# A four-layer convolution chain: first gram matrix from row loads and transposes, second image's gram rows two steps later, and final loads placed in the stages' own tiles

## The chip, the cores and the metric

The kernel runs on one core of one Trainium2 chip. The metric is the device time of one execution in microseconds (us); lower is better. Everything is float32.

## The reference

The input x has 16 images of 64 channels and 128 x 128 pixels. Four layers follow one another, each of the form x = x + layer(groupnorm(x)), with 32 groups of 2 channels:

```python
# layer 0: gram matrix per image, then a 1x1 convolution
gram = jnp.einsum('bcn,bdn->bcd', xf, xf) / N          # xf: (B, C, H*W), N = H*W
y = jnp.einsum('bcd,bdn->bcn', gram, xf)
out = jnp.einsum('oc,bchw->bohw', conv_w, y)
# layer 1: two fixed 3x3 edge filters per channel
out = jnp.abs(y[:, 0]) + jnp.abs(y[:, 1])
# layer 2: shift a quarter of the channels left, a quarter right, then a 3x3 convolution plus bias
# layer 3: 3x3 convolution, 1x1 convolution, batch norm over ALL images, leaky relu
y = (y - mean) * jax.lax.rsqrt(var + EPS)
return jnp.clip(jnp.where(y >= 0, y, LEAK * y), 0.0, CEIL)
```

Two facts order the whole program. The gram matrix of an image needs all of that image before layer 0 can start on it. The batch norm of layer 3 needs all sixteen images before the last element-wise pass can start on any of them.

## The kernel before, in words

Every image passes through four stages, each a small class whose method `at(i, q)` issues the work for row block i (8 of them, each 8 rows of both image halves) in quarter q of a step.

- `Gram` (lines 407 to 444) computes the gram matrix. It loads x with pixels on the partitions (`xr`, eight loads of 512 KB in runs of one 128-pixel row, 512 bytes), ScalarE copies each into `xw`, and TensorE takes 128 products of 64 x 65 from `xw`. Then `gram_chain` (lines 301 to 405) runs some fifty tiny operations that end in the mixing matrix `abd` and the normalisation numbers `co` of layer 1.
- `Front` (lines 450 to 566) loads x again in rows (`x`, two loads of 256 KB per block, 4 KB runs), mixes it with `abd` on TensorE (`po`), normalises it into `xh` on ScalarE, does layer 1 on VectorE (`u`, `e`) and stores x2 to device memory.
- `Layer2` (lines 625 to 770) loads x2 back (`v2`), forms differences and products, and stores x3 (`x3_d`). The x3 tiles stay on chip too: ten buffers named `x3`.
- `Layer3` (lines 773 to 857) uses the x3 tiles, forms differences, products and y, accumulates the sums for the batch norm, and stores y (`y_d`, four stores of 128 KB per block from a ring of two `y` tiles).

The order is written out by hand: `keep_in_program_order` (line 72) keeps every instruction of the five engine wrappers in the order in which Python issues it, so each engine has one fixed list. The line of almost all instructions in the profile is therefore 72, and groups are told apart by tile names. The order of steps stands in lines 861 to 900: `starts` sets Front, Layer2 and Layer3 of image b at steps 15 + 8b, 25 + 8b and 35 + 8b (with some lead), and `pace` sets `Gram`: image 0 from step 0, images 1 to 6 at double speed from step 12 on, every fourth step, later images every eighth. `tick` advances the small chains by one link each quarter step.

SP issues almost all transfers, from one list in program order. The transfers rotate over eight completion semaphores, and in the built program each transfer waits for the one eight before it.

After the last stage all pools are closed. The batch norm's numbers follow (lines 905 to 928: `mv`, `pm_bn`, ..., `sc`, `sh`), and then the end: a new pool `io` with six buffers each of `yt` and `rt`, 64 parts of 1 MB, four of them loaded ahead:

```python
    for n, (b, q) in enumerate(parts):
        fetch(n + 4)
        yt, rt = loaded.pop(n)
        act.activation(yt, yt, AF.Relu, bias=sh, scale=sc)
        dve.scalar_tensor_tensor(rt, yt, 255.0, rt, op0=ALU.min, op1=ALU.add)
        sp.dma_start(whole(out[b].rearrange("c h w -> (c h w)"), q), rt)
```

Of the kernel before, what the change touches and what calls it, by code (L numbers as in the profile page):

```python
# [9 lines left out]
F32 = mybir.dt.float32  # L10
# [5 lines left out]
P = 128  # L16
# [91 lines left out]
def tile_kernel(ctx: ExitStack, tc: tile.TileContext, x, cw_h, w2_t, b2, wbin_t, w1_t, b1, gamma, beta, consts, out):  # L108
# [9 lines left out]
    nc.sync.dma_start(kc, consts)  # L118
# [4 lines left out]
    def load_const(src, shape, name):  # L123
        t = cpool.tile(shape, F32, name=name)
        nc.sync.dma_start(t, src)
        return t

    cwh = load_const(cw_h, [P, C], "cwh")
    b2_sb = load_const(b2, [P, 1], "b2_sb")
    b1_sb = load_const(b1, [P, 1], "b1_sb")  # L130
    gamma_sb = load_const(gamma, [P, 1], "gamma_sb")
    beta_sb = load_const(beta, [P, 1], "beta_sb")
# [24 lines left out]
    with ExitStack() as ph:  # L157
        wpool = ph.enter_context(tc.tile_pool(name="wpool", bufs=1))
        xin = ph.enter_context(tc.tile_pool(name="xin", bufs=2))
        work = ph.enter_context(tc.tile_pool(name="work", bufs=2))  # L160
        ring = ph.enter_context(tc.tile_pool(name="ring", bufs=2))
        stp = ph.enter_context(tc.tile_pool(name="stp", bufs=2))
        ps_two = ph.enter_context(tc.tile_pool(name="ps_two", bufs=2, space=PSUM))
        ps_one = ph.enter_context(tc.tile_pool(name="ps_one", bufs=1, space=PSUM))
        ps_po = ph.enter_context(tc.tile_pool(name="ps_po", bufs=1, space=PSUM))
        ps_g = ph.enter_context(tc.tile_pool(name="ps_g", bufs=1, space=PSUM))
        ps_sm = ph.enter_context(tc.tile_pool(name="ps_sm", bufs=1, space=PSUM))

        def sv(name, n=1):
            return small.tile([P, n], F32, tag=name, name=name)  # L170

        def cols(o):
            return slice(o * C, (o + 1) * C)

        last = [1]

        def small_product(dst, wt, src):

            for o in (1 - last[0], last[0]):
                pe.matmul(dst[cols(o)], wt[:, cols(o)], src, start=True, stop=True)  # L180
            last[0] = o


        bank = ps_sm.tile([P, 512], F32, name="bank")
        turn = [0]

        def sm(n, rows=P):
            if n > 8:
                return bank[0:rows, P:P + n]
            turn[0] = (turn[0] + 1) % 16  # L190
            return bank[0:rows, 8 * turn[0]:8 * turn[0] + n]
# [3 lines left out]
        xw = wpool.tile([P, W // 2, C + 1, 2], F32, name="xw")  # L195
        nc.gpsimd.memset(xw[:, :, C, :], 1.0)

        xh = wpool.tile([P, 3, R + 2, W + 2], F32, name="xh")
        nc.gpsimd.memset(xh, 0.0)
        junk = wpool.tile([P, R * W], mybir.dt.bfloat16, name="junk")  # L200
        wbd = wpool.tile([P, P], F32, name="wbd")
        nc.gpsimd.memset(wbd, 0.0)

        w2 = wpool.tile([P, 3, 3, P], F32, name="w2")
        w3 = wpool.tile([P, 3, 3, P], F32, name="w3")
        nc.gpsimd.memset(w2, 0.0)
        nc.gpsimd.memset(w3, 0.0)
        for slot, i, o, ky in TO_SLOTS:
            nc.scalar.dma_start(w2[i * C:(i + 1) * C, slot, :, o * C:(o + 1) * C], w2_t[:, ky])

        wm = wpool.tile([P, 3, P], F32, name="wm")
        for n in range(2):
            o = 1 - single(TO_SLOTS, n)[0]
            nc.vector.tensor_copy(wm[:, :, cols(o)], w2[:, n, :, cols(o)])
        w0 = wpool.tile([P, P], F32, name="w0")
        nc.gpsimd.memset(w0, 0.0)

        wb = work.tile([P, R + 1, W + 2], F32, tag="u", name="wb")
        wb = flat(wb)[0:C, 0:9 * C].rearrange("p (y x c) -> p y x c", y=3, x=3)
        w1 = work.tile([P, R, W + 2], F32, tag="e", name="w1", bufs=1)[0:C, 0, 0:C]  # L220
        nc.scalar.dma_start(wb, wbin_t)
        nc.scalar.dma_start(w1, w1_t)
        for ky in range(3):
            pw = sm(3 * C, rows=C).rearrange("p (k c) -> p k c", k=3)
            for kx in range(3):
                nc.tensor.matmul(pw[:, kx, :], wb[:, ky, kx, :], w1, start=True, stop=True)
            for slot, i, o, kk in TO_PAIRS:
                if kk == ky:
                    nc.vector.tensor_copy(w3[i * C:(i + 1) * C, slot, :, o * C:(o + 1) * C], pw)

        packed = {}
        for name, w, table in (("pk2", w2, TO_SLOTS), ("pk3", w3, TO_PAIRS)):
            nc.vector.tensor_add(w[:, 2], w[:, 0], w[:, 1])
            packed[name] = wpool.tile([P, 2, C], F32, name=name)
            for n in range(2):
                o, i = single(table, n)
                for kx, half in ((1, i), (0, 1 - i)):
                    nc.vector.tensor_copy(
                        packed[name][half * C:(half + 1) * C, n], w[i * C:(i + 1) * C, n, kx, o * C:(o + 1) * C]
                    )  # L240

        diffs, twins = {}, {}
        for name in ("d2", "d3"):
            diffs[name] = wpool.tile([P, 2, CP, W + 2], F32, name=name)
            nc.gpsimd.memset(diffs[name], 0.0)
            twins[name] = wpool.tile([P, 2, CP, W + 2], F32, name=f"q{name}")
            nc.gpsimd.memset(twins[name], 0.0)


        chains = []  # L250

        def tick():
            for c in list(chains):
                if next(c, chains) is chains:
                    chains.remove(c)

        def rstd(mE, eps):

            me = sv("me", 2)
            dve.tensor_copy(me, mE)  # L260
            nv = sv("nv")
            dve.scalar_tensor_tensor(nv, me[:, 0:1], me[:, 0:1], me[:, 1:2], op0=ALU.mult, op1=ALU.subtract)
            var = sv("var")
            dve.tensor_scalar(var, nv, -1.0, eps, op0=ALU.mult, op1=ALU.add)
            sd = sv("sd")
            act.activation(sd, var, AF.Sqrt)
            yield
            r0 = sv("r0")
            dve.reciprocal(r0, sd)

            e = sv("e")
            dve.scalar_tensor_tensor(e, var, r0, r0, op0=ALU.mult, op1=ALU.mult)
            dve.tensor_scalar(e, e, -0.5, 1.5, op0=ALU.mult, op1=ALU.add)
            r = sv("r")
            dve.tensor_mul(r, r0, e)
            return r, me[:, 0:1]

        def coefficients(st, put, back=None):

            s2 = sv("s2", 2)  # L280
            dve.tensor_reduce(s2, st, axis=AX.X, op=ALU.add)
            yield
            pm = sm(2)
            small_product(pm, k("gmean"), s2)
            yield
            r, mean = yield from rstd(pm, GN_EPS)
            co = sv("co", 2) if back is None else sv("co2", 6)
            dve.tensor_copy(co[:, 0:1], r)
            dve.scalar_tensor_tensor(co[:, 1:2], mean, -1.0, r, op0=ALU.mult, op1=ALU.mult)
            if back is not None:  # L290

                dve.reciprocal(co[:, 2:3], r)
                dve.tensor_mul(co[:, 3:4], co[:, 2:3], k("left"))
                dve.tensor_mul(co[:, 4:5], co[:, 2:3], k("right"))
                dve.tensor_add(co[:, 5:6], mean, back)
            put(co)


        lead = {}

        def gram_chain(b, pg):

            gs = stp.tile([P, C + 1], F32, tag="gs", name=f"gs_{b}", bufs=1)
            dve.tensor_copy(gs, pg)
            if b > 1:
                yield
            gd = sm(C + 1)
            small_product(gd, k("same"), gs)
            yield
            g = stp.tile([P, C + 1], F32, tag="g", name=f"g_{b}", bufs=1)  # L310
            dve.tensor_scalar_mul(g, gd, 1.0 / HW)
            mu = g[:, C:C + 1]
            st = sv("st0", 2)
            dve.tensor_copy(st[:, 0:1], mu)
            junk0 = stp.tile([P, C], F32, tag="junk0", name=f"junk0_{b}", bufs=1)
            dve.scalar_tensor_tensor(
                junk0, g[:, 0:C], 1.0, k("Id"), op0=ALU.mult, op1=ALU.mult, accum_out=st[:, 1:2]
            )
            if b > 1:
                yield  # L320
            pm = sm(2)
            small_product(pm, k("gavg"), st)
            yield
            r, mean = yield from rstd(pm, GN_EPS)
# [7 lines left out]
            if b > 1:  # L332
                yield
# [660 lines left out]
```

## Time and profile before

| what | value |
|---|---|
| median of three runs | 2853.81 us (2851.17 to 2856.24) |
| the profiled execution's own time | 2855.78 us |
| its span, first to last instruction | 2854.0 us |
| TensorE busy | 2238.3 us (78% of the span) |
| VectorE busy | 2193.6 us (77%) |
| ScalarE busy | 2101.5 us (74%) |
| GpSimd busy | 886.8 us (31%) |
| bytes moved by DMA | 685.91 MB, mean 240 GB/s |
| granted TensorE clock, mean | 0.893 |

The page cuts the span into 40 slices of 71 us; each digit is the busy share of a slice in tenths. The chain of waits is followed back from the last instruction to whatever released each step. A window's row gives the busy time of each engine in one stretch, the granted TensorE clock, the mean share of the 16 DMA engines, and GB/s. PE is TensorE's matmul, PEld its weight load, DVE VectorE, ACT ScalarE, POOL GpSimd, SP SyncE.

### The profile page before, as it was taken

How to read it: one execution, taken by the hardware profiler on the slowest of the kernel's cores; microseconds unless marked ns; L12 is line 12 of the kernel's file. 1: busy time of each engine (PE TensorE's matmuls, PEld its weight loads, DVE VectorE, ACT ScalarE, POOL GpSimd, SP SyncE). 2: the span in 40 equal slices, each digit the busy share in tenths (PEclk: the TensorE clock that was granted, in tenths of full speed). 3: DMA queues.
4: the chain of work that ended last, by engine and by line, in shares of the span. 5: the costliest groups of instructions: out<-in, count | busy, mean ns of one | idle time of the engine just before them, and what ended most of it. 6: DMA issues, size and time to landing. Idle time of an engine off the chain costs nothing. (4 is left out here: it accounts for less than half of the span.)

```text
span 2854.0 us, 45849 instructions
## 1 busy us (share of the span) xinstructions
PE 2238.3 (78%) x14772; PEld 1166.6 (41%) x14772; DVE 2193.6 (77%) x3694; ACT 2101.5 (74%) x3107; POOL 886.8 (31%) x1326
## 2 busy tenths in 40 slices
PE   3568899999999999999999999999999992000000
PEld 2333444545463635363635453566666640000000
DVE  3999999898989898989898989999995333332332
ACT  4666779888889898888898979899996674222222
POOL 1045434343434343434333434444443300000000
PEclk8678999999999999999999999999999996555555
DMA  6788978888888888888888867888877528999999
GB/s 164 191 221 225 234 199 239 215 224 215 220 216 221 218 221 217 216 216 216 220 220 217 214 178 193 211 209 209 211 199 185 145 71 320 426 426 426 426 426 394
DMA packets 661229, 685.91 MB, mean 240 GB/s; under 512 B 58672, under 2 KB 587072, under 8 KB 636416
## 3 DMA queue, kind: packets, MB, share of 16 engines
q1 hardware_dynamic: 635008, 614.41, 72.7%
q0 software_dynamic: 24576, 68.12, 9.8%
q8 instruction: 119, 1.95, 0.3%
q14 instruction: 118, 0.97, 0.1%
q10 hardware_dynamic: 1408, 0.46, 0.1%
HBM read 346.23 MB, written 268.44 MB: 215 GB/s over the span
## 5 line engine op out<-in xcount | busy, mean ns | idle before, releaser
L72 PE MATMUL two<-d,w 128*64 128x508 f32 (+2 forms) x2560 | 890.5, 586 | 0.0
L72 PE MATMUL two<-d,wi 128*64 128x508 f32 (+3 forms) x1536 | 619.7, 577 | 0.0
L72 POOL DMA_DIRECT2D qd<-d x512 | 270.3, 530 | 868.9 <-issue 312.7
L72 PE MATMUL two<-qd,pk 128*64 128x512 f32 (+1 forms) x1024 | 518.9, 588 | 6.3 <-DMA qd<-d 5.8
L72 POOL TENSOR_SCALAR edges<-v,co 64x8 f32<-64x8 f32 x512 | 355.3, 694 | 358.9 <-ACT v L72 266.7
L72 PEld LDWEIGHTS two<-d,w 128*64 128x64 f32 x2560 | 306.2, 136 | 275.7 <-issue 188.8
L72 PE MATMUL po<-x,abd 128*64 128x512 f32 x1024 | 367.9, 628 | 56.9 <-ACT xh L72 55.9
L72 DVE TENSOR_TENSOR d<-v 128x512 f32<-128x512 f32 (+1 forms) x512 | 346.8, 680 | 76.2 <-issue 36.9
L72 DVE SCALAR_TENSOR_TENSOR rt<-yt,rt 128x2048 f32<-128x2048 f32 x64 | 146.7, 2292 | 321.3 <-DMA rt<-x_d 321.3
L72 PE MATMUL one<-v,w 128*64 128x508 f32 (+2 forms) x1600 | 392.7, 578 | 0.0
L72 PE MATMUL one<-v,wi 128*64 128x508 f32 (+3 forms) x1536 | 391.1, 593 | 0.0
L72 ACT ACTIVATE yt<-yt,sh,sc 128x2048 f32<-128x2048 f32 x64 | 134.1, 2095 | 332.7 <-DMA yt<-y_d 332.7
L72 ACT COPY qd<-d 64x512 f32<-64x512 f32 x512 | 316.0, 617 | 20.9 <-DVE d L72 14.5
L72 DVE SCALAR_TENSOR_TENSOR e<-e 128x1032 f32<-128x1032 f32 (+1 forms) x256 | 313.4, 1224 | 0.0
L72 ACT ACTIVATE xh<-po,co 128x128 f32<-128x128 f32 (+1 forms) x480 | 275.6, 622 | 39.5 <-PE po L72 37.4
L72 PEld LDWEIGHTS two<-d,wi 128*64 128x64 f32 x1536 | 195.8, 135 | 145.8 <-issue 96.3
L72 DVE SCALAR_TENSOR_TENSOR y<-two,c 128x1024 f32<-128x1024 f32 x128 | 156.1, 1220 | 122.7 <-ACT v L72 65.7
L72 POOL TENSOR_SCALAR v<-v,kc 128x9 f32<-128x9 f32 x256 | 245.1, 971 | 12.0
L72 PEld LDWEIGHTS one<-v,w 128*64 128x64 f32 x1600 | 172.7, 137 | 157.1 <-issue 92.6
L72 ACT ACTIVATE v<-x,co 128x512 f32<-128x512 f32 (+2 forms) x368 | 235.6, 707 | 0.0
L72 PEld LDWEIGHTS one<-v,wi 128*64 128x64 f32 x1536 | 164.9, 139 | 152.4 <-issue 106.4
L72 ACT ACTIVATE u<-u 128x1024 f32<-128x1024 f32 x128 | 135.7, 1060 | 96.1 <-DVE u L72 95.8
(136 smaller groups left out, 3455.2 us busy)
## 6 DMA issues: line engine op xcount, KB each, us to landing
xr<-in_x SPq DMA_DIRECT2D x128, 512.0 KB, 6.9
x<-in_x SPq DMA_DIRECT2D x256, 256.0 KB, 4.2
x_d<-u SPq DMA_DIRECT2D x512, 128.0 KB, 3.6
y_d<-y SPq DMA_DIRECT2D x512, 128.0 KB, 4.2
yt<-y_d SPq DMA_DIRECT2D x64, 1024.0 KB, 16.2
rt<-x_d SPq DMA_DIRECT2D x64, 1024.0 KB, 12.3
out<-rt SPq DMA_DIRECT2D x64, 1024.0 KB, 14.4
x_d<-x SPq DMA_DIRECT2D x496, 128.0 KB, 2.5
```

The source lines that it names most:

```text
L72: return self.tc.keep_in_program_order(call(*args, **kwargs))
```

## The change

Three parts, and what they need.

1. The first image's gram matrix. `first_gram` runs ahead of the step loop. It loads image 0 in rows (4 KB runs) into eight of the ten `x3` buffers, turns 64 blocks of 128 x 128 on TensorE with the identity, copies the results from PSUM into `xw` (one half on VectorE, one on ScalarE), takes the 128 gram products block by block, and runs the whole `gram_chain` with nothing between its links. The weights of layer 3 are made after the fourth block, the other derived weights after the chain. The constants' loads move to the GpSimd queue, except for the identity, which is first on SP's. The step loop now begins at step 12.
2. `pace` starts at image 1 and step 14, so the gram stages of images 1 to 6 come two steps later; from image 7 on they stay. One link of the chain of image 1 no longer waits for a tick.
3. The end. The pools stay open. The parts are 512 KB (N = R * W, 4 KB runs per partition), 128 of them, and their tiles are the stages' own: 38 tiles or slices (`xw`, `xh`, `x`, `xr`, `u`, `e`, `v2`, `d2`, `qd2`, then `x3`, `y`, `v3`), which `rest` and `slices` add to `room`. From the first step of the last image's layer 3 on, each quarter step may `fetch` one pair. In the final loop a pair is reused once more than eight tiles are free.

```diff
-    nc.sync.dma_start(kc, consts)
+    sp.dma_start(kc[:, 0:P], consts[:, 0:P])
+    pool.dma_start(kc[:, P:K_END], consts[:, P:K_END])
...
+    def first_gram():
...
+        for m in range(NS):
+            t = ring.tile([P, 2, CP, W], F32, tag="x3", name=f"x_first_{m}", bufs=NS + 2)
+            t = t.rearrange("p a j w -> p (a j w)")
+            for h in range(2):
+                sp.dma_start(t[h * C:(h + 1) * C], halves(x[0].rearrange("c h w -> (c h w)"), h, m * R, R))
+            src.append(t)
+        for m in range(NS + 1):
+            if m < NS:
+                two = ps_two.tile([P, 2, CP, W], F32, tag="two", name=f"turned_{m}").rearrange("p a j w -> p (a j) w")
+                for j in range(R):
+                    pe.transpose(two[:, j], src[m][:, j * P:(j + 1) * P], k("I"))
+                for h, copy in ((0, dve.tensor_copy), (1, act.copy)):
+                    copy(xw[:, m * R:(m + 1) * R, 0:C, h], two[:, :, h * C:(h + 1) * C])
+            if m > 0:
+                for w in range(2 * R * (m - 1), 2 * R * m):
+                    gram_product(pg, w)
+            if m == 3:
+                weights_of_layer_3()
+        for _ in gram_chain(0, pg):
+            pass
+        other_weights()
...
-        for b in range(B):
-            half = 1 <= b <= 2 * EARLY
-            pace[b] = at, 2 if half else 1
-
-            at += (NS // 2 if half else NS) + {0: 4, 2 * EARLY: 2}.get(b, 0)
-        for step in range(8 * (B - 1) + 35 + NS + 1):
+    first_gram()
+    at = 14
+    for b in range(1, B):
+
+        pace[b] = at, 2 if b <= 2 * EARLY else 1
+        at += NS // pace[b][1]
+    last_one = NS * (B - 1) + starts[0][1]
+    N = R * W
...
+    def fetch():
+        n = fetched[0]
+        if n < len(parts):
+            b, q = parts[n]
+            yt, rt = room.popleft(), room.popleft()
+            sp.dma_start(yt, whole(y_d[b], q))
+            sp.dma_start(rt, whole(x3_d[b], q))
+            loaded.append((yt, rt))
+            fetched[0] += 1
+
+    for step in range(starts[2][1] - 3, steps):
...
+            if step == last_one and q == 0:
+                slices(xw.rearrange("p w c t -> p (w c t)"), 8)
+                slices(xh.rearrange("p a j w -> p (a j w)"), 3)
...
+            if step >= last_one and q == 2:
+
+                n = 3 if step == last_one else 1 if step < last_one + NS - 2 else 0
+                rest(ring, "x3", [2, CP, W], NS + 2, n)
+            if step >= last_one and len(room) > 1:
+                fetch()
+    while chains:
+        tick()
+    rest(ring, "x3", [2, CP, W], NS + 2, NS + 2 - 3 - (NS - 3))
+    rest(ring, "y", [2, CP, W], 2)
+    rest(ring, "v3", [R + 1, W], 2)
+    while len(room) > 1:
+        fetch()
...
-    N = 16 * W
-    for n in range(4):
-        fetch(n)
-    for n, (b, q) in enumerate(parts):
-        fetch(n + 4)
-        yt, rt = loaded.pop(n)
+    for b, q in parts:
+        yt, rt = loaded.popleft()
         act.activation(yt, yt, AF.Relu, bias=sh, scale=sc)
         dve.scalar_tensor_tensor(rt, yt, 255.0, rt, op0=ALU.min, op1=ALU.add)
         sp.dma_start(whole(out[b].rearrange("c h w -> (c h w)"), q), rt)
+        room.extend((yt, rt))
+
+        if len(room) > 8:
+            fetch()
```

## The prediction

> **What bounds the kernel now.** I read the 40 slices first, then the chain of waits, then the windows of the stretches that the change touches.
>
> ```profile
> PE   3568899999999999999999999999999992000000
> DMA  6788978888888888888888867888877528999999
> DMA out<-rt 15%; PE two L72 1%; DMA rt<-x_d 1%; PE one L72 0%; SPq L72 0%; ACT qd L72 0%; ACT junk L72 0%; DVE rt L72 0%; DVE y L72 0%; DVE d L72 0%; ACT c L72 0%; PE pm_bn L72 0%; DVE var_bn L72 0%; DVE mv L72 0%; ACT sd_bn L72 0%
> ```
>
> There are three regimes. Five slices of ramp (71 us each) have TensorE partly idle. From about 200 to 2370 us TensorE is at 9; the change leaves the products there alone. The last seven slices have TensorE at 0 and the DMA at 9: the chain sees only `out<-rt`. The slices before them are the chance: TensorE is full, the DMA nearly empty. Busy times below are us (xcount) of PE, PEld, DVE, ACT, POOL, then clock, DMA share, GB/s:
>
> ```profile
> 6.10:27.30 21.20, 2.67 (x18) 2.14 (x18) 6.78 (x18) 10.58 (x10) 4.23 (x7) 1.00 0.97 242
> 27.30:39.00 11.70, 9.76 (x256) 9.56 (x256) 0.04 (x1) 1.21 (x1) 0.00 (x0) 1.00 0.71 178
> 39.00:51.00 12.00, 5.93 (x46) 3.18 (x46) 7.21 (x45) 1.80 (x4) 0.00 (x0) 0.72 0.00 1
> 2301.00:2371.00 70.00, 67.76 (x278) 22.39 (x275) 22.74 (x46) 53.30 (x90) 0.00 (x0) 1.00 0.27 68
> 2376.00:2840.00 464.00, 0.00 (x0) 0.00 (x0) 144.39 (x63) 133.63 (x64) 0.00 (x0) 0.50 1.01 425
> ```
>
> Start: 21 us of short-packet loading (ACT's copies wait for `xr`), 12 us of gram, 12 us of chain with only tiny operations. End: 464 us at 425 GB/s, which nothing but fewer bytes or a better rate shortens. Between them, 70 us at 68 GB/s.
>
> The timeline dates the first image's coefficients and its first Sobel operation:
>
> ```profile
> 38.96 0.23 DVE L72 COPY gs<-pg 128x65 f32<-128x65 f32 x1 [22.84 <-PE pg L72]
> 50.88 0.13 DVE L72 COPY co<-me 128x1 f32<-128x1 f32 x1
> 60.85 1.38 DVE L72 SCALAR_TENSOR_TENSOR u<-xh 128x1170 f32<-128x1170 f32 x1 [9.84 <-ACT xh L72]
> ```
>
> [...] The trace agrees in the one short window that the first image's row loads (4 KB packets) have nearly to themselves; the end stage with 8 KB packets holds 426:
>
> ```profile
> 2.75:4.25 1.50, 0.00 (x0) 0.00 (x0) 0.00 (x0) 0.00 (x0) 1.50 (x2) 1.00 1.02 369
> 110.25:110.50 0.25, 0.25 (x4) 0.00 (x0) 0.21 (x3) 0.11 (x2) 0.08 (x1) 0.50 0.99 410
> 2400.00:2800.00 400.00, 0.00 (x0) 0.00 (x0) 123.76 (x54) 111.92 (x54) 0.00 (x0) 0.50 1.01 426
> ```
>
> [...] The kernel before has no transpose.
>
> **The change, part by part.**
>
> *First gram.* Eight `xr` loads in 512-byte packets and eight ACT copies (1.15 us each, waiting on them) go. In come 16 loads of 256 KB in 4 KB packets, 64 transposes, and 8 copies of 128x512 each on DVE and ACT side by side (about 0.7 us; nearest rows: 680 ns on DVE, 773 on ACT), hidden under the next tile's transposes. SP issues them at 0.59 us each (9.5 us), ahead of their arrival. Estimated loading: 4.2 MB, plus 0.75 MB of constants on POOL's queue beside it, at 400 GB/s is 12 us; first tile about 5.0 us, last about 16.5. TensorE: [...] I take 160, so 64 x 0.16 = 10.2 us. The gram's 256 passes stay, 9.8 us. Layer 3's weights are now inside TensorE's order after tile 3: three rounds of product and DVE copies, 1.8 us a round before (6.61 to 8.38), so 4 us with the last overlapping. Last copy 0.9. Sum: 5.0 + 10.2 + 9.8 + 4.0 + 0.9 = 29.9 us against 38.9. The chain after it is already alone before (39.0 to 50.9) and keeps its 12 us, so "alone" earns nothing. Remaining weight copies (some 4 us of DVE) now follow the chain, hidden by the 10 us in which ACT and PE fill `xh`. POOL's memsets and loads have those 30 us. Gain 9 us; [...] at 314 ns, a loss of 1.
>
> *Second image two steps later.* Before, ACT copies three `xw` chunks ahead of the first `xh` (until 52.7, 1.8 us after `co`). Now the first `xr` is issued on SP behind x_2, which waits for the first mix, so ACT's copies may wait some 1.6 us for it behind `xh`, delaying the first absolute values. I take +1 net. Images 1 to 6 move two steps, 7 and later stay: the same work. The second image's chain now ends one quarter step before it is needed; DVE, the bound there, issues it in order, so 0, at worst -2. Start in all: +10 (-3 to +17), carried through, since every later instruction is in fixed order.
>
> *End.* 64 parts of 1 MB become 128 of half that: ACT 64 x 2095 ns becomes about 128 x 1060, DVE 128 x 1180, far under the DMA time. Bytes are unchanged (201.3 MB), packets shrink from 8 to 4 KB. There are 38 tiles, 19 pairs. In program order 16 pairs (16.8 MB) are issued on SP between layer 3's last stores; at 407 GB/s that is 41 us, with 4.2 MB of y stores (16 us at 68/0.27 = 250 GB/s) 57 us in a 70 us stretch. The last three pairs wait for the last x3, y and v3 tiles, about 2373.5, where loads begin today; batch-norm's scale (2375) then finds data.
>
> From 2373.5, before: 201.3 MB at 425.5 is 473 us and 7 of fill and tail, to 2854. After: 184.5 MB at 407 is 453, and 5: 458 against 480, **22 us**. Preloading alone is worth 39 us at today's rate; shorter packets give back 20. At 426 the gain is 42, at 395, 8.
>
> What SP queues behind the preloads is the y stores. Each waits for the eighth transfer before it, so up to 4 MB, 10 us, lie ahead; y has two buffers and is rewritten two steps (15.6 us) later. About 14 us of that is left after DVE wrote it, so I cost this at 0; if the cover goes, DVE's `y` waits, then `two` and TensorE, up to 3 us in each of 3 crowded steps: 9 us.
>
> **Sum.** 10 + 22 = 32 us off the profiled execution's 2855.8 (span 2854.0). That execution lies 2 us above the median and within the runs' 2851 to 2856, so I take the same difference from 2853.8: **2822**. A measurement tells about 0.2%, 5.7 us, from no change.
>
> **Rivals.**
> - *4 KB packets cost nothing* (12%): for it, DMA share is 1.01 at 426 and longer packets may have nothing to amortize; against it, the 410 window. 2853.8 - 10 - 42 = 2802.
> - *The start earns nothing* (14%): transposes near 314 ns, TensorE still at the half clock (0.50 in windows around it), or late `xr`. Against it: the loads finish by 16.5. 2853.8 - 22 = 2832; with y's stores late too, 2841.
> - *Slower: the end's DMA rate* (8%). One mechanism: twice the packets over 470 us. It decides at 184.5/(480 + 10 - 5) = 380 GB/s. The constants' load (rows of 4.9 KB, 128 partitions) shows 369 between 2.75 and 4.25; then 184.5/0.369 = 500 + 5, 25 more than before, less 10: 2869. Against it: tiny constants ran among those packets.
> - *The preloads do not run early* (5%): were a tile's release late, SP would block until the stages end; 201.3 MB at 407 is 495 + 5, 20 more, less 10: 2864, or equal when partly early. Against it: every stage of images up to 15 that owned those tiles, but layer 3, has ended by then in program order.
>
> **How the numbers follow.** The likeliest case has 61%, within 2811 to 2834 (395 to 415 GB/s, start 5 to 14). The range 2796 to 2846 adds the first two rivals and late stores, leaving the slow ones out. Faster by over 0.2%: 61 + 12 + 14 = 87%; within 0.2%: 4% (the last rival, partly early); slower: 8 + 1 = 9%.
>
> **What would show it.** Right: the gram's copy to `gs` near 30 us and the first `u` near 50; over 200 GB/s in the slices of layer 3's last image with TensorE still at 9; `out` stores starting within 3 us of batch-norm's shift; a steady end at 400 to 410 GB/s, some 435 to 460 us long. Wrong: an end steady under 380 or at 426; DVE `y` waiting on DMA in the last image; transposes over 0.3 us apiece; a middle stretch (200 to 2200 us) whose length moves by more than 3 us.

## The result, and the profile after

| | time, us | ratio to before, 95% interval |
|---|---|---|
| before | 2852.49 median of 4 (2851.01 to 2856.24) | |
| after | 2836.96 median of 4 (2834.40 to 2840.61) | 0.9945 [0.9927, 0.9962] |

The change makes the kernel 15.5 us faster. It was forecast as faster, but by 32 us, so half of the expected gain is missing. The profiled execution of after took 2840.6 us (span 2838.8), 3.6 us above its median; its span is 15.2 us shorter than that of before.

First the 40 slices, then the chain of waits of after. TensorE is still at 0 in the last slices, but the DMA now rises one slice earlier, and the chain's last stretch is divided among the stages' own tiles:

```profile
PE   5577899999999999999999999999999995000000
DMA  6699987888888888888888877888887668999999
GB/s 151 171 220 238 221 225 215 209 226 210 222 207 228 207 227 209 229 207 228 212 221 215 220 186 195 206 212 208 215 208 188 157 192 295 419 420 420 420 420 385
DMA out<-end_x 2%; DMA end_x<-x_d 2%; DMA xw<-y_d 1%; DMA end_x<-y_d 1%; DMA xw<-x_d 1%; DMA end_y<-y_d 1%; DMA qd<-x_d 1%; DMA end_xr<-x_d 1%; DMA out<-end_u 1%; DMA out<-end_v 1%; DMA end_e<-y_d 1%; DMA d<-y_d 0%; DMA out<-xw 0%; DMA out<-end_xr 0%; DMA end_u<-x_d 0%; DMA end_u<-y_d 0%
```

The timeline of after dates the same three operations as before, from the gram's copy to the first Sobel operation:

```profile
36.44 0.23 DVE L73 COPY gs<-pg 128x65 f32<-128x65 f32 x1 [1.95 <-PE pg L73]
49.02 0.13 DVE L73 COPY co<-me 128x1 f32<-128x1 f32 x1
57.28 1.38 DVE L73 SCALAR_TENSOR_TENSOR u<-xh 128x1170 f32<-128x1170 f32 x1 [5.18 <-ACT xh L73]
```

The first `u` stood at 60.85 before. The start has gained 3.6 us here, not 10.

Two windows of after, from the last image's first `y` to its last, and in the steady end. The columns are busy us (xcount) of PE, PEld, DVE, ACT, POOL, then clock, DMA share, GB/s:

```profile
2325.46:2386.17 60.71, 56.24 (x222) 18.27 (x218) 17.07 (x28) 41.16 (x68) 0.00 (x0) 0.97 0.84 305
2400.00:2800.00 400.00, 0.00 (x0) 0.00 (x0) 140.60 (x116) 141.95 (x116) 0.00 (x0) 0.50 1.03 420
```

The preloads run where they should: 305 GB/s under layer 3. But the stretch takes 60.7 us, against 54.8 at 67 GB/s before:

```profile
2314.56:2369.35 54.79, 54.41 (x222) 18.08 (x218) 17.07 (x29) 41.24 (x68) 0.00 (x0) 1.00 0.27 67
```

The end holds 420 GB/s.

**Where the time went**, by setting the same operation of both traces side by side (every `u<-xh` and `y<-two` has a fixed place in DVE's order):

| stretch | before, us | after, us | difference |
|---|---|---|---|
| start to first `u` | 60.85 | 57.28 | -3.6 |
| first `u` to first `y` of the last image | 2253.7 | 2268.2 | +14.5 |
| first to last `y` of the last image | 54.8 | 60.7 | +5.9 |
| last `y` to the end of the span | 484.65 | 452.63 | -32.0 |

So the end gained more than forecast. The middle, costed at 0, lost 14.5 us, and layer 3 lost 5.9. Between 270 and 500 us the middle loses 18; some 3 come back later.

DVE's waits in the ramp of after (57 to 520 us; line waited for: us in total, times, longest) put a name on the middle's loss:

```profile
DVE me L73 <- PE bank L73: 14.8, 4, 7.2
DVE gs L73 <- PE pg L73: 9.1, 5, 2.6
```

`me` is the copy of the group statistics in `rstd`. The kernel before has no such wait between 260 and 520 us; its longest sums there are these:

```profile
DVE d L72 <- POOL v L72: 4.8, 8, 1.6
DVE d L72 <- issue: 2.8, 1, 2.8
DVE gs L72 <- PE pg L72: 2.4, 2, 1.8
```

The longest wait for `me`, in the timeline of after:

```profile
275.99 5.36 PE L73 MATMUL one<-v,wi 128*64 128x512 f32 x12
...
283.22 0.23 PE L73 MATMUL bank<-st,kc 128*64 128x2 f32 x2
...
284.05 0.22 PE L73 MATMUL bank<-st,kc 128*64 128x2 f32 x2
...
284.31 0.16 DVE L73 COPY me<-bank 128x2 f32<-128x2 f32 x1 [7.18 <-PE bank L73]
```

The two halves of the statistics' product (`bank<-st,kc`) stand in TensorE's order behind layer 2's `one` and part of its `two`; `me` is next in DVE's order, so DVE does nothing for 7.2 us.

DVE's waits in the last image's layer 3 of after (2325 to 2390 us):

```profile
DVE y L73 <- DMA y_d<-y: 15.3, 2, 9.0
DVE y L73 <- DMA end_x<-y_d: 6.8, 1, 6.8
```

`y` waits for its own tile to be stored, 15.3 us in two waits. From issue to landing, the stores took a median of 2.4 us before and of 6.0 in after (2300 to 2370 us of each trace):

```profile
y_d<-y SPq DMA_DIRECT2D x36, 128.0 KB, 2.4
y_d<-y SPq DMA_DIRECT2D x28, 128.0 KB, 6.0
```

The waits are longer than the loss, since DVE idles for 5.4 us between `y` and `y` in any case.

### The profile page after: what moved, and what is told of

Same layout as the page of the kernel before. It is cut to its first block, busy times and chain, and to the rows that moved or that the text cites. A ratio compares the mean times of both kernels' runs of the same rounds, so it can differ in the third digit from the quotient of the medians.

```text
span 2838.8 us, 46440 instructions
## 1 busy us (share of the span) xinstructions
PE 2259.0 (80%) x14836; PEld 1176.0 (41%) x14836; DVE 2204.6 (78%) x3767; ACT 2115.0 (75%) x3171; POOL 888.2 (31%) x1340
## 3 DMA queue, kind: packets, MB, share of 16 engines
q8 instruction: 120, 1.97, 0.3%
## 5 line engine op out<-in xcount | busy, mean ns | idle before, releaser
L73 POOL TENSOR_SCALAR edges<-v,co 64x8 f32<-64x8 f32 x512 | 343.1, 670 | 358.3 <-ACT v L73 211.9
L73 PE MATMUL po<-x,abd 128*64 128x512 f32 x1024 | 372.0, 633 | 59.1 <-ACT xh L73 59.1
L73 PEld LDWEIGHTS po<-x,abd 128*64 128x64 f32 x1024 | 111.4, 141 | 176.8 <-ACT xh L73 98.9
L73 DVE SCALAR_TENSOR_TENSOR u<-xh 128x1170 f32<-128x1170 f32 x128 | 175.5, 1371 | 7.1 <-ACT xh L73 5.2
```

The costliest lines, as they stand in the source:

```text
L73: return self.tc.keep_in_program_order(call(*args, **kwargs))
```

## The experiments

All are timed in five rounds against the kernel before. "Expected" was written before each ran.

| kernel | median, us | ratio, 95% interval |
|---|---|---|
| pace12 | 2825.11 | 0.9896 [0.9882, 0.9909] |
| old_start | 2826.90 | 0.9901 [0.9888, 0.9915] |
| late_chain | 2828.97 | 0.9917 [0.9904, 0.9931] |
| two_pairs | 2831.45 | 0.9917 [0.9904, 0.9931] |
| y_on_act | 2833.14 | 0.9931 [0.9919, 0.9944] |
| none_early | 2872.80 | 1.0061 [1.0048, 1.0075] |
| late_weights | 2834.14 | 0.9931 [0.9919, 0.9943] |
| combined | 2812.61 | 0.9855 [0.9841, 0.9868] |
| short_packets | 2816.33 | 0.9866 [0.9850, 0.9883] |
| rows128 | 2809.73 | 0.9846 [0.9831, 0.9860] |

One thing has to be known to read single traces: five kernels that share after's start code have their first `u` at 57.28 (after), 53.71, 55.51, 53.34 and 54.41 us. The trace of after has the latest start of them, and `gs` in the same five lies between 33.2 and 36.4. So stretches are compared from the first `u` on, and differences of totals under 3 us, or of `gs` under some 3 us, are not leaned on. Before's median also moved with the rounds, from 2852.5 (those of after) to 2855.0 (those of pace12), so a difference between two kernels of different rounds is given by their ratios too where it matters.

### The pace of images 1 to 6: pace12 and old_start

```
-    at = 14
+    at = 12
...
-        at += NS // pace[b][1]
+        at += NS // pace[b][1] + (2 if b == 2 * EARLY else 0)
```

> The kernel after, with images 1 to 6's gram steps at 12, 16, ... 32 as in the kernel before (two steps earlier than after), image 7 again at 38. Start and end as after. Theory (the delay of two steps moved gram work out of the idle start into the loaded stretch where layer 2 and layer 3 begin, and costs the 14.5 us that the alignment loses between 280 and 500 us): about -14, 2823 us; first y of the last image near 2311 instead of 2325. Rival (the loss has another cause: the shorter start merely shifts the phase and the ramp waits for something else, such as DMA): 2837 within 3. Second rival (the rows of image 1 then delay the first u by what the start gained, 3.6 us): 2827.

Measured: 2825.1, 12 us under after (14 by the two ratios); the last image's first `y` at 2308.05. DVE's waits of pace12 in its ramp no longer hold `me`:

```profile
DVE d L73 <- POOL v L73: 7.8, 11, 1.6
DVE gs L73 <- PE pg L73: 7.3, 5, 1.9
DVE u L73 <- ACT xh L73: 6.9, 1, 6.9
```

The two later steps cost the middle's time. The second rival has a part in it: from `gs` to the first `u` is 22.6 us here (34.55 to 57.11) and 20.8 in after, because ACT again makes image 1's copies there. In the single traces the delay is worth 1.7 us at the start and costs 17 later, since from the first `u` to the last image pace12 is even 2.8 us faster than before; the totals show 12 to 14 as the balance.

old_start also puts the first image's gram back to 512-byte packets, while constants and weights keep after's order of loading:

```
-    first_gram()
+    weights_of_layer_3()
+    other_weights()
...
-    at = 14
-    for b in range(1, B):
+    at = 0
+    for b in range(B):
...
-        at += NS // pace[b][1]
+        at += NS // pace[b][1] + {0: 4, 2 * EARLY: 2}.get(b, 0)
...
-    for step in range(starts[2][1] - 3, steps):
+    for step in range(steps):
...
-            for b in range(1, B):
+            for b in range(B):
```

> The kernel after with the start of before: image 0's gram from 512-byte packets in the same steps as before, images 1 to 6 two steps earlier, the constants' loads in after's order; end as after. Theory (start gained 3.6, pace lost 14.5): 2837 + 3.6 - 14.5 = 2826 us. Rival (the pace costs nothing, the middle's loss comes from the end's tiles or from what the scheduler changed): 2841 us.

Measured: 2826.9, as the theory has it. But it also showed what I had not expected, in the gram's copy of old_start:

```profile
35.17 0.23 DVE L73 COPY gs<-pg 128x65 f32<-128x65 f32 x1 [11.21 <-PE pg L73]
```

With the old gram it comes at 35.2; with transposes in the five traces at 33.2 to 36.4; in the kernel before at 39.0. So old_start's `gs` lies among those of the transposes, and before's does not. As far as single traces can tell, what the start had gained came mostly from moving the constants' and weights' loads to POOL (with the reordering that belongs to the same edit), and not from long packets.

### Products or chains: late_chain

```
-                chains.append(gram_chain(b, self.pg))
+                chains.append(later(gram_chain(b, self.pg), 8 if 2 < b <= 2 * EARLY else 0))
```

(`later` yields eight times, two steps, before the chain begins.)

> The kernel after, its rows, copies and gram products at the same steps, but the gram chains of images 3 to 6 begin two steps (eight quarters) later. Theory (what costs the middle 14.5 us is not the moved products but where the chains fall: four times DVE's me copy waits, 14.8 us in all, for the chain's statistics product, which TensorE reaches only behind layer 2's and layer 3's products): the waits on me under 3 us, the last image's first y near 2312 instead of 2325, 2824 us. Rival (the moved products and row copies themselves load TensorE and the DMA engines when these are full): 2837 within 3, the waits gone to other rows.

Measured: 2829.0, 8 us under after, between the two; the two ratios' intervals still touch, so the stretch has to decide. From the first `u` to the last image, relative to before, after and the four others with its pace (two_pairs, y_on_act, none_early, late_weights) lose 13.0 to 14.5 us, late_chain 5.6. DVE's waits of late_chain in the ramp:

```profile
DVE u L73 <- ACT u L73: 7.3, 5, 2.8
DVE d L73 <- POOL v L73: 6.6, 7, 2.3
DVE gs L73 <- PE pg L73: 6.3, 2, 4.0
DVE two L73 <- PE two L73: 3.7, 2, 1.9
```

The waits on `me` are gone and about 8 of the 14 us with them: that part is where the chains' steps fall in TensorE's order. The other 6 are spread over waits on ACT, POOL and `two`. They go with the pace (pace12). They may belong to row copies and products two steps later, or to the chains at their new place; no run separates these, and it stays open which of them it is.

### The stores of the last image: two_pairs and y_on_act

two_pairs loads two pairs of tiles a step, after the stores:

```
-            if step >= last_one and len(room) > 1:
+            if step >= last_one and q in (1, 2) and len(room) > 1:
```

> The kernel after, but in layer 3's last image only two pairs of the end's tiles are loaded per step, right after the y stores and one quarter later, in place of one in each quarter. Theory (y's stores wait on SP behind four pairs of loads): DVE's y no longer waits on DMA, the last image's layer 3 takes 55 us instead of 61, the end's start finds nearly as many tiles: 2831 us. Rival (the loads slow the stores merely by sharing the DMA engines, or the loads left out come back at the end): 2837 or up to 2845.

y_on_act leaves the loads and moves the stores' issue to another engine:

```
-                                sp.dma_start(v[:, z], y[s * C:(s + 1) * C, z])
+                                (act if b == B - 1 else sp).dma_start(v[:, z], y[s * C:(s + 1) * C, z])
```

> The kernel after, with the y stores of the last image issued by ACT in place of SP; the tiles' loads as in after. Theory (the stores are late because SP issues them behind the loads): the stall of 6 us in layer 3 goes, 2831 us. Rival (they are late because 16.8 MB of loads share the DMA engines with them): the stall stays, 2837 us.

The window from first to last `y`, of two_pairs and then of y_on_act:

```profile
2320.80:2375.56 54.76, 54.38 (x222) 18.39 (x218) 17.07 (x29) 41.15 (x68) 0.00 (x0) 1.00 0.96 330
```

```profile
2321.45:2380.58 59.13, 56.18 (x222) 18.50 (x218) 17.08 (x29) 41.16 (x68) 0.00 (x0) 0.97 0.93 331
```

Both move bytes at 330 GB/s. With two pairs a step the stretch is as short as before; a store lands in 3.1 us (median). With the stores on ACT's queue it is still 4.3 us longer than before, and the stores land in 6.1 us (median of 28 from 2300 to 2370 us, 20 of them issued by ACT). DVE's waits of y_on_act there:

```profile
DVE y L73 <- PE two L73: 23.2, 4, 7.1
DVE y L73 <- DMA y_d<-y: 13.4, 2, 7.8
```

(Of the first line, 5.4 us in each of the four are the idle time that is there in any case.) The same stretch takes 58.9 to 63.2 us in the other kernels with one pair a quarter step and the stores on SP (after, pace12, old_start, late_chain, late_weights), so y_on_act's 59.1 shows no gain, and the order of issue on SP is not the main cause. Of the two causes put up, this leaves the rival's, that the stores share the DMA engines with the loads in flight (a DMA share of 0.93 there, against 0.27 before); no run shows it by itself. two_pairs met its theory's 2831 all the same, at a share of 0.96. It halves the loads of a step and also puts them right behind the stores; no run separates these two. y_on_act's total, 2833.1, lies between the two expectations and can't decide, since its ratio's interval overlaps that of after; the stretch in question does.

### What the preloads are worth: none_early

```
-            if step >= last_one and len(room) > 1:
-                fetch()
```

> The kernel after, with no tile of the end loaded before layer 3 has ended; all 19 pairs are asked for then. Theory (preloading is worth its bytes at the end's steady rate, 16 pairs of 1 MB at 420 GB/s = 40 us, less the 6 us stall it causes): 2837 + 40 - 6 = 2871 us, 18 slower than the kernel before, since the tiles and the start alone give little. Rival (the end's rate or the longer tail is what gained): 2850 or less.

Measured: 2872.8, as the theory has it, and slower than before. The steady end of none_early:

```profile
2400.00:2800.00 400.00, 0.00 (x0) 0.00 (x0) 132.50 (x109) 133.87 (x109) 0.00 (x0) 0.50 1.03 419
```

From its last `y` (2376.95) to the end (2870.2) are 493.3 us, against 484.7 before: tiles of half the size with 4 KB packets, and more of them in use, cost **8.6 us** net over the same bytes. Against after's 452.6, early loading earns **40.7 us**.

### The start: late_weights, combined, short_packets, rows128

late_weights makes layer 3's products in a PSUM tile of their own after the chain's first product, and copies them after the chain (the new tile inside `weights_of_layer_3` is left out here):

```
...
-            if m == 3:
-                weights_of_layer_3()
-        for _ in gram_chain(0, pg):
-            pass
+        made = weights_of_layer_3()
+        for n, _ in enumerate(gram_chain(0, pg)):
+            if n == 0:
+                next(made)
+        for _ in made:
+            pass
```

> The kernel after, with layer 3's weight products out of the first gram: they are made beside the chain in a tile of their own, their copies after the chain. Theory (they hold TensorE 3.6 us and drop its clock for 6 us more): gs near 31.5 instead of 36.4, the first u 5 us earlier, 2832 us. Rival (the gram is held by the rows' arrival, the last near 27): gs near 34, first u 2 us earlier, 2835 us.

TensorE's timeline in after around these products shows what they cost:

```profile
17.76 1.10 PE L73 MATMUL turned<-kc,x_first 128*128 128x128 f32 x8
18.79 1.22 PE L73 MATMUL pg<-xw 128*64 128x65 f32 x32
19.94 0.56 PE L73 MATMUL bank<-w,wb 64*64 64x64 f32 x6
21.38 0.56 PE L73 MATMUL bank<-w,wb 64*64 64x64 f32 x6 [0.88 <-DVE w L73]
22.75 0.90 PE L73 MATMUL bank<-w,wb 64*64 64x64 f32 x6 [0.81 <-DVE w L73]
23.57 1.97 PE L73 MATMUL turned<-kc,x_first 128*128 128x128 f32 x8
25.47 2.00 PE L73 MATMUL pg<-xw 128*64 128x65 f32 x32
```

They hold TensorE 3.6 us (19.94 to 23.57), and the next groups take 1.97 and 2.00 us in place of 1.10 and 1.22; the granted clock is 0.54 between 22 and 28 us, and 1.00 there in late_weights and in combined, which has the products at the same place. In the four other traces with after's start code the copies of the two tiles behind the products start 2.2 us apart, against 3.8 in after: of the five traces only after's has the slower groups. In late_weights both are gone, and its `gs` is at 32.07, though two of its tiles now wait for their rows (0.58 and 1.30 us). Against after that is 4.4 us earlier, but against the mean of the four other traces (33.74) only 1.7, and the five differ by 3.3 among themselves. The total, 2834.1, lies between the two expectations (2832 and 2835), and its ratio's interval overlaps that of after. So what the weights' place costs the whole kernel stays open.

combined takes pace12, two_pairs and late_weights together, and has the constants (but the identity) and the weights loaded behind the first image's rows:

```
-    pool.dma_start(kc[:, P:K_END], consts[:, P:K_END])
-    for t, src in ((wb, wbin_t), (w1, w1_t), (cwh, cw_h)):
-        pool.dma_start(t, src)
...
             src.append(t)
+        sp.dma_start(kc[:, P:K_END], consts[:, P:K_END])
+        for t, d in ((cwh, cw_h), (wb, wbin_t), (w1, w1_t)):
+            sp.dma_start(t, d)
```

(POOL's loads of biases and `w2` move behind its memsets.)

> Images 1 to 6 at 12, 16, ... as in pace12, two pairs a step as in two_pairs, layer 3's weights as in late_weights, and all constants but the identity and all weights loaded after the first image's rows. Theory (the terms add: 14 of the pace, 6 of the stores, 5 of the weights, 2 to 4 of the loads): 2837 - 28 = 2809 us, gs near 29. Rival (the start binds elsewhere, the rows' arrival or the chain): 2818 us.

Measured: 2812.6, `gs` at 27.92. The terms add up but for 3.6 us of the forecast, so the theory's 2809 is nearer than the rival's 2818; the first `u` is at 51.01, 23.1 after `gs`, with image 1's copies in between. With nothing else loading, the rows still came at 238 to 240 GB/s between 6 and 15 us, with the DMA share over 1. Two runs ask why. short_packets takes `first_gram()` out of combined again, as old_start does, with the constants' loads issued at step 8 and the weights made at step 12:

```
+            if (step, q) == (8, 0):
+                sp.dma_start(kc[:, P:K_END], consts[:, P:K_END])
...
+            if (step, q) == (12, 0):
+                for _ in weights_of_layer_3():
+                    pass
+                other_weights()
```

> The kernel combined, with the first image's gram from 512-byte packets and ACT copies as in the kernel before, the constants still behind the rows. Theory (the long packets by transposes bring nothing: the rows of 64 partitions load at about 245 GB/s in either size, and what the start gained came from the constants and weights moved away): gs within 3 us of combined's 27.9, total 2813 within 3, ratio near 0.986. Rival (short packets are slower once nothing else loads beside them): gs 5 us later or more, 2818 us or more.

Measured: `gs` 5.7 us later and 2816.3. At `gs` the rival holds: with the rest out of the way, transposes do beat short packets. The total, 3.7 us above combined, lies between the two, and the intervals of the ratios overlap.

rows128 loads each tile by one transfer of 128 partitions:

```
-            for h in range(2):
-                sp.dma_start(t[h * C:(h + 1) * C], halves(x[0].rearrange("c h w -> (c h w)"), h, m * R, R))
+            sp.dma_start(t, x[0].rearrange("c (h n) w -> (c h) (n w)", h=2)[:, m * R * W:(m + 1) * R * W])
...
-                    copy(xw[:, m * R:(m + 1) * R, 0:C, h], two[:, :, h * C:(h + 1) * C])
+                    copy(xw[:, m * R:(m + 1) * R, 0:C, h], two.rearrange("p j (c h) -> p j h c", h=2)[:, :, h])
```

> The kernel combined, with each tile of the first image's rows loaded by one transfer of 128 partitions (channel and half) in place of two of 64, the halves sorted out by the copies behind the transposes. Theory (64 partitions per transfer set the 240 GB/s): near 400 GB/s while rows load, the last tile some 7 us earlier, TensorE then binds and gs comes near 25.5 instead of 27.9, 2810 us. Rival (the rate is that of 4 KB packets from these addresses, whatever the partitions): 240 GB/s again, gs unchanged, 2812.6 us.

Windows while the rows load, of combined and then of rows128, and `gs` of rows128:

```profile
6.00:9.00 3.00, 2.67 (x12) 2.33 (x13) 0.69 (x1) 0.22 (x1) 3.00 (x5) 1.00 1.05 240
```

```profile
6.00:9.00 3.00, 3.00 (x19) 2.67 (x19) 0.94 (x2) 0.63 (x1) 3.00 (x5) 1.00 1.03 421
9.00:12.00 3.00, 3.00 (x52) 2.75 (x50) 0.77 (x2) 0.65 (x1) 3.00 (x6) 1.00 1.02 415
```

```profile
25.26 0.23 DVE L73 COPY gs<-pg 128x65 f32<-128x65 f32 x1 [1.96 <-PE pg L73]
```

The same 4 KB packets from the same addresses go at 421 GB/s instead of 240, `gs` comes at 25.3, and the kernel takes **2809.7 us**, 44 less than before and 27 less than after. (Against combined alone, the intervals of the ratios overlap; the windows decide here.) TensorE now binds this stage: it is busy without a gap from 6 to 22 us. What the run doesn't separate is the number of partitions from the size of a transfer, 512 KB instead of 256.

## Why the prediction was right, and where it was wrong

It was right on the sign, and the median lies in its range; it lies outside the likeliest case's own range (2811 to 2834), because four terms of the sum were off, in both directions. That it lies in the range is in part luck: losses of 27 us against the forecast met 10 more at the end.

- **Start, +10 us forecast.** After's trace shows 3.6; the four other traces of the same start 5.3 to 7.5. Of the forecast's 9 us to `gs`, after's trace has 2.5. "First tile about 5.0 us" was 9.41. With the constants and weights loaded behind the rows (combined) it was 6.07, and with 128 partitions a transfer (rows128) 5.07, so most of that miss was the constants' and weights' loads on POOL's queue, and the shape of the transfers came second:

```profile
9.41 1.94 PE L73 MATMUL turned<-kc,x_first 128*128 128x128 f32 x8 [9.41 <-DMA x_first<-in_x]
6.07 1.94 PE L73 MATMUL turned<-kc,x_first 128*128 128x128 f32 x8 [6.07 <-DMA x_first<-in_x]
5.07 3.64 PE L73 MATMUL turned<-kc,x_first 128*128 128x128 f32 x16 [5.07 <-DMA x_first<-in_x]
```

  I took 400 GB/s for the rows, an estimate of mine with only a quarter of a microsecond at 410 behind it. That window was too short to carry it: the same trace has 295 GB/s from 110 to 111 us and 229 from 111 to 112. As transfers of 64 partitions the rows, with what loads beside them, got 251 in after's window of 9 to 12 us, and rows128, with 421 and 415 against combined's 240 and 238, shows that the shape of the transfer sets it. Transposes at "160" ns were 191 on average (12.2 us for 64), and the gram's passes took 11.3 us instead of 9.8. The weights' "4 us" were 3.6, but no term was there for the slower groups behind them in after's trace (0.9 and 0.8 us for those next to them). The last copy's 0.9 was almost all hidden.
- **The chain, 12 us unchanged**: right (36.44 to 49.02 is 12.6, with the alone part earning nothing).
- **"I take +1 net" for the second image's rows at the start**: right in sign and near in size. Copies that are not there gained 1.7 us (20.8 from `gs` to `u` against pace12's 22.6).
- **"The same work ... so 0, at worst -2" for the two later steps: the step that failed.** It cost 14.5 us in the trace; undoing it gives 12 to 14 (pace12). The argument counted work and the last deadline of the second image. It did not set the moved steps of images 3 to 6 against the steps that they now stand behind in TensorE's order. By step 25 layer 2 runs, and a 0.23 us product waits in its queue while DVE waits for it. I had named the sign of this ("a middle stretch whose length moves by more than 3 us") without pricing it as a rival. Some 8 of the 14 us are shown to be the chains' place (late_chain); the cause of the rest is open.
- **Preloading, "39" us**: right, 40.7.
- **Shorter packets "give back 20"**: too much; 8.6. The mis-sized term is the rate: 407, an estimate of mine with the same short window behind it, stood for a steady stream that runs at 420, against 426 with the longer packets.
- **Stores behind the preloads, 0, or 9 if the cover goes**: the cover went, at 5.9 us, within the bounds given, and the sign named for it, `y` waiting on DMA in the last image, came. The mechanism named, SP's order of issue, is not the main one: in y_on_act 4.3 us stay without it. What was measured is that beside the loads in flight the stores land in 6.0 us (6.1 with most of them on ACT's queue) instead of 2.4; how the loads delay them is not shown.
- **Transposes, "160" ns apiece**: an estimate of mine; the kernel before has no transpose to show it, and its nearest row, a 128x128 pass of `bank<-kc,vv`, took 314 ns on average. Groups of eight took 1.10 us, 0.14 each, or 1.94 to 1.97, 0.24 each, at the start and after the pause.
- **A slip in reading the slices**: the last six have TensorE at 0 and the DMA at 9, not seven; the sum does not use it.

By the traces: of the 32 forecast, 10 more at the end, 6 less at the start, 14.5 lost in the middle and 5.9 under layer 3 leave 15.

The rivals: "4 KB packets free" was nearly right on its own term (8.6 instead of 20 or 0); "slower end rate" and "preloads not early" are excluded by 420 and 305 GB/s. "The start earns nothing ... with y's stores late too, 2841" came nearest in number (2837.0 measured), but only half for its own reasons: y's stores were late, yet the start did earn 3.6 us, the end earned 32 instead of 22, and the middle's loss is not in it.

## What to carry to other kernels

In this kernel every engine has one fixed list. There, work moved to a later step is not free merely because its amount is the same: look at what it now stands behind on each engine, and above all at small operations that another engine waits for (DVE's four waits on `me`, 14.8 us, were for products of 0.23 us). Price an early load by the traffic it shares the DMA engines with: the same bytes at two pairs a step, right behind the stores, cost nothing here (54.8 us for the last image's layer 3, as before), while one pair a quarter step cost 5.9. And before shortening packets or lengthening them, look at how many partitions a transfer spans and how large it is, which rows128 changed together (from 240 to 421 GB/s).

## What the runs showed of the hardware

- 256 KB loads with 4 KB rows into 64 partitions: 238 to 240 GB/s with a DMA share of 1.04 to 1.06 (combined, 6 to 15 us). 512 KB loads with the same rows into 128 partitions: 415 to 421, at 1.02 to 1.03 (rows128, 6 to 12 us). A DMA share near 1 does not tell that the rate is at its best.
- Stores of 0.5 MB a step land in 2.4 us alone (before), 3.1 with two 1 MB pairs of loads a step (two_pairs) and 6.0 with up to four (after; medians), though the bytes moved in the stretch hardly differ: 54.8 us at 330 GB/s and 60.7 at 305.
- A group of eight 128 x 128 transposes took 1.10 us, and 1.97 in after behind the weights' products, where the granted clock was 0.54 (22 to 28 us); in late_weights and combined it stayed at 1.00 there and the groups at 1.06 to 1.10. The four other traces of after's start code show no slower groups there. The first group of after took 1.94 us at a granted clock of 1.00 (9 to 12 us).
- The start varies between executions: the first `u` of five kernels with the same start code lay between 53.3 and 57.3 us.
